# Transposing the attention probabilities of every second head pair on VectorE and through SBUF-to-SBUF transfers

## The chip, the cores and the metric

The kernel runs on one core of one Trainium2 chip. The metric is the device time of one execution in microseconds (us); the median of three runs of the kernel before is 1169.73 us (1169.29 to 1170.1).

## What is computed

A batch of four sequences of 512 tokens with 1024 features goes through a layer norm, a causal attention of 16 heads with rotary positions, and a gate from a feed-forward part with sign weights; the product of both is added to the input. Cut to the attention, which the change touches:

```python
xn = _layernorm(x, axis=-1)
q, k, v = ((xn @ w).reshape(b, s, 16, 64) for w in (Wq, Wk, Wv))
q, k = rotary(q), rotary(k)
logits = jnp.where(causal, einsum('bhqd,bhkd->bhqk', q, k), MASK_VAL) / 8
attn = softmax(logits, axis=-1)
out = einsum('bhqk,bhkd->bhqd', attn, v).reshape(b, s, e) @ Wo
...
x + out * silu(ffn(xn))
```

## The kernel before

**Units and groups.** A unit is a pair of heads of one sequence: 64 rows of q and k per head, 128 together. Two units make a group; there are four groups per sequence, 16 in all (`groups`, L225), numbered k = 0 to 15, with g = k mod 4 the place of a group in its sequence. The order of the work on TensorE (PE) is written out by hand (`manual_schedule`, L70). The order on the other engines is made by the framework's planner from the dependencies, with the order in which the instructions are traced as the priority. An instruction under `keep_in_program_order` is pinned behind the instruction of its engine that was traced just before it.

**The main loop** (L879 to L952) goes through the 16 groups. In the time of group k, PE does the projections of that group (queries, keys, values, each by a seven-product scheme; `fill`, a generator that gives one matmul at a time, 84 per group) and, between them, the attention of group k - 1. `interleave` (L870) takes a list of pieces, traces one, and then draws so many matmuls from `fill` that both lists end together: with 16 pieces that is 5.25 matmuls a piece. `attention_pieces` (L839) makes the list. In groups g = 2 and 3 the next sequence's layer norm is traced ahead of the pieces (`layernorm`, L915) and the transposes of its tokens are put among them (`extra`, L916). The first operations of the next sequence's sums (`form_x`, L298) are traced between the last group of one sequence and the first of the next (L951).

**Scores and softmax.** For the block row i of 128 queries, a score matmul (`scores`, L512) makes 128 x 128(i+1) logits per head in PSUM. VectorE (DVE) adds the mask on the diagonal block and takes the negated maximum (L528, L532), ScalarE (ACT) takes the exponential with the row sum (L535), VectorE the reciprocal (L543), and GpSimd (POOL) multiplies by it in place (L545). The score banks are `ps_sc`, two tiles of two banks each. `scores_1` does block row 1 of both units, `scores_3` row 3, `scores_02` rows 2 and 0. The probabilities lie in separate tiles for the rows 1, 3 and 2 with 0 (`new_probs`, L553), with 3, 2 and 2 buffers.

**Transposes and values.** The product with v needs the probabilities with keys on the partitions. `transpose_p` (L577) transposes four 128x128 blocks on PE into one PSUM bank; the five banks of a unit (20 blocks, `T_BANKS`) are copied to the tile `pT` by ScalarE (banks 0, 2, 4; L589) or VectorE (banks 1, 3; L587). `pT` comes from `ptp` (L144), a pool with one buffer. `values` (L591) then runs eight matmuls, VectorE copies the result from PSUM (L608), and a DMA issued on SyncE's queue (SP) stores it (L609). All banks of projections, transposes and values come from one ring of four PSUM banks (`ring`, L134).

**The order of the pieces.** `late` holds the two units of group k - 2, `w` and `v`: their scores were done in group k - 1's time, and their transposes and values are done in group k's. It is empty for k = 1. The list is five transposes of `w`; `scores_1` of the newer pair with the values of `w`; five transposes of `v`; `scores_3` with the values of `v`; a wait; `scores_02`; two waits (L858). The router's three steps (L617) are put in for g = 0.

**Queues.** Loads of weights and tokens, stores of tokens and values, and the router's small stores all stand in SP's queue, each behind its own waits.

**After the loop** (L1046 to L1094) the last two pairs' attention is mixed by hand with the feed-forward's matmuls (`dense`, L1050) and with `split` (L758), which works on ScalarE and VectorE. The rest, from 885 us on, is output projection and feed-forward, which the change leaves alone.

Of the kernel before, what the change touches and what calls it, by code (L numbers as in the profile page):

```python
# [9 lines left out]
F32 = mybir.dt.float32  # L10
# [10 lines left out]
B, S, E = 4, 512, 1024  # L21
H, D = 16, 64
NE = 8
P = 128
NT = B * S
NC = E // P
NPAIR = H // 2
NGRP = NPAIR // 2
TPB = S // P
# [4 lines left out]
SCALE = 0.125  # L34


T_BANKS = [
    [(0, 0, i) for i in range(4)],
    [(1, 0, i) for i in range(4)],
    [(0, 1, 1), (0, 1, 2), (0, 1, 3), (0, 3, 3)],  # L40
    [(1, 1, 1), (1, 1, 2), (1, 1, 3), (1, 3, 3)],
    [(0, 2, 2), (0, 2, 3), (1, 2, 2), (1, 2, 3)],
]


def t_place(h, j):

    return [(h, 0), (2 + h, 0), (4, 256 * h), (2 + h, 384)][j]


@with_exitstack
def attn_gated_ffn_kernel(
# [15 lines left out]
    nc = tc.nc  # L68
# [8 lines left out]
    ident = cp.tile([P, P], F32, name="ident")  # L77
# [4 lines left out]
        out=mask,  # L82
        in_=mask,
# [18 lines left out]
    osc = cp.tile([P, E], F32R, name="osc")  # L102
# [3 lines left out]
    for sign, base in ((1, 0), (-1, 7)):  # L106
        nc.gpsimd.affine_select(
            out=high,
# [45 lines left out]
    def bank(name):  # L154
        return ring.tile([P, S], F32, tag="r", name=name)
# [349 lines left out]

    def probs(u, i):

        if i % 2:
            return PR[u, i]
        return PR[u, 0][:, :, P * i // 2 : P * i // 2 + (i + 1) * P]  # L510

    def scores(blocks):  # L512

# [36 lines left out]
    def sc_bank(u, n):  # L550
        return ps_sc.tile([P, 2, S], F32, tag="sc", name="sc_%d_%d_%d_%d" % (*u, n))

    def new_probs(u, n, cols, bufs):  # L553
        PR[u, n] = pp.tile(
            [P, 2, cols], F32, tag=f"p{n}", name="p%d_%d_%d_%d" % (n, *u), bufs=bufs
        )

    def scores_1(units):
        ps = sc_bank(units[0], 1)
        for u in units:  # L560
            new_probs(u, 1, 2 * P, 3)
        scores([(u, 1, ps[:, :, n * TH : (n + 1) * TH]) for n, u in enumerate(units)])

    def scores_3(units):
        for u in units:
            new_probs(u, 3, S, 2)
        scores([(u, 3, sc_bank(u, 3)) for u in units])

    def scores_02(units):
        blocks = []  # L570
        for u in units:
            new_probs(u, 0, S, 2)
            ps = sc_bank(u, 0)
            blocks += [(u, 2, ps[:, :, P:]), (u, 0, ps[:, :, :P])]
        scores(blocks)

    def transpose_p(u, n):  # L577
        un = "%d_%d_%d" % u
        if u not in PT:
            PT[u] = ptp.tile([P, 5, S], F32, tag="pT", name=f"pT_{un}")  # L580
        tp = tp_bank(f"ptp_{un}_{n}")
        for k, (h, j, i) in enumerate(T_BANKS[n]):
            nc.tensor.transpose(tp[:, k, :], probs(u, i)[:, h, j * P : (j + 1) * P], ident)  # L583
        dst = PT[u][:, n, :]
        src = tp.rearrange("p j q -> p (j q)")
        if n % 2:
            nc.vector.tensor_copy(dst, src)  # L587
        else:
            nc.scalar.copy(dst, src)  # L589

    def values(u):  # L591
        b, g, i = u
        pr = g + NGRP * i
        pv = bank("pv_%d_%d_%d" % u)
        for j in range(TPB):
            for h in range(2):
                r = h * D
                n, o = t_place(h, j)
                nc.tensor.matmul(  # L599
                    pv[r : r + D, j * P :],  # L600
                    lhsT=V[u][:, j, r : r + D],
                    rhs=PT[u][:, n, o : o + (TPB - j) * P],
                    start=(j == 0),
                    stop=(j == TPB - 1),
                )

        at = V[u].rearrange("p t c -> p (t c)")
        nc.vector.tensor_copy(at, pv)  # L608
        nc.sync.dma_start(  # L609
            out=at_d[b].rearrange("t p (c q) -> p t c q", c=NC)[:, :, pr, :],  # L610
            in_=at.rearrange("p (t q) -> p t q", t=TPB),
        )


# [224 lines left out]
    def attention_pieces(k, late):  # L839

        units = [(*groups[k], i) for i in range(2)]
        w, v = late

        def pt(u):
            return [lambda n=n: transpose_p(u, n) for n in range(5)] if u else []

        def with_values(scores_of, u):
            def both():
                scores_of(units)
                if u:  # L850
                    values(u)

            return both

        def wait():
            pass

        pieces = [  # L858
            *pt(w),
            with_values(scores_1, w),  # L860
            *pt(v),
            with_values(scores_3, v),
            wait,
            lambda: scores_02(units),
            wait,
            wait,
        ]
        return pieces, units

    def interleave(pieces, fill, n_fill):  # L870
# [8 lines left out]
    for k, (b, g) in enumerate(groups):  # L879
# [4 lines left out]
        if g == 0:  # L884
            routing = [lambda n=n: router(b, n) for n in range(3)]
            if k == 0:
                nothing = lambda: None
                pieces = [
                    routing[0],
                    lambda: (load_scales(in_scale), load_scales(out_scale)),  # L890
                    routing[1],
                    nothing,
                    routing[2],
                    lambda: split_scales(isc),
                    nothing,
                    nothing,
                    nothing,
                ]
            else:

                if b < B - 1:
                    pieces.insert(7, routing[0])
                pieces.insert(10, routing[1])
                pieces.insert(13, routing[2])
        elif g == 1 and b + 1 < B:

            pieces.insert(12, lambda: [load_x(b + 1, t) for t in range(2)])
            if b == 0:
                pieces.insert(6, lambda: split_scales(osc))

                pieces.insert(1, lambda: None)
        elif g > 1 and b + 1 < B:
            t0 = 2 * (g - 2)
            for t in range(t0, t0 + 2):
                layernorm(b + 1, t)  # L915
            extra = [  # L916
                lambda t=t, h=h: transpose_x(b + 1, t, h) for t in range(t0, t0 + 2) for h in range(2)
            ]
            if g == 2:
                extra.append(lambda: [load_x(b + 1, t) for t in (2, 3)])  # L920

        step = max(1, (len(pieces) + len(extra)) // (len(extra) + 1))
        for n, e in enumerate(extra):
            pieces.insert(min(len(pieces), (n + 1) * step + n), e)
        if len(pieces) > 18:

            pieces.append(lambda: None)
        if k in (5, 9, 12, 13):
            n = {5: 0, 9: 2, 12: 4, 13: 6}[k]
            pieces.insert(8, lambda: make_sign(n + 1))  # L930
# [116 lines left out]
    w, v = late  # L1047
    sums = iter([(n, c) for n in (1, 3) for c in range(4)])

    def dense(gates, n):  # L1050
        for _ in range(n):
            next(gates)
            if n > 1:
                nxt = next(sums, None)
                if nxt:
                    sum_wo(*nxt)

    for n in range(5):
        transpose_p(w, n)
    split(0, 0)  # L1060
    scores_1(units)
    split(0, 1)
    values(w)
    gates = gated(0)
    for ns in ((0, 1), (2, 3), (4,)):
        dense(gates, 2)
        for n in ns:
            transpose_p(v, n)
    scores_3(units)
    values(v)  # L1070
    dense(gates, 6)

    split(1, 0)
# [348 lines left out]
```

## Time and profile before

| | |
|---|---|
| median of three runs | 1169.73 us |
| the profiled execution | 1170.42 us, its span 1168.6 us |
| granted TensorE clock | 0.998 |
| PE busy in the span | 1159.0 us |
| DVE, ACT, POOL busy in the span | 826.0, 496.8, 559.8 us |
| projections on PE, share of the chain that ended last | L342 31%, L429 15% |
| transposes of probabilities, scores, values, share of the chain | 6%, 6%, 6% |
| DVE, ACT, POOL busy in the group from 354 to 406 us | 37.7, 27.7, 26.6 us of 52 |
| bytes moved by DMA | 121.92 MB, mean 104 GB/s |

The span is the time from the first to the last instruction on the core. PE is TensorE's matmul side and PEld its weight loads. A row of the groups names the line, the engine, the operation and the tiles (out<-in with shapes and a count), then the busy time in total, the mean duration of one in ns, and the idle time of the engine just before. A row of the timeline gives the start, the length and the merged instructions. A row of waits gives who waited for whom, with the sum, the number and the longest. A float32 matmul stands as two instructions in the trace, a transpose as one. Numbers like 128x256 are partitions by elements.

### The profile page before, as it was taken

What the parts mean: (1) busy time and instruction counts of PE and PEld (TensorE: products, weight loads), DVE (VectorE), ACT (ScalarE), POOL (GpSimd) and SP (SyncE); (2) the same over time, 40 slices, a digit from 0 to 9 for tenths busy, and PEclk for the clock granted to TensorE, in tenths of its full rate; (3) what the DMA queues carried; (4) which work ended last, traced back from release to release, by engine and by line L of the source; (5) the groups of instructions that cost most, each with busy time, mean ns of one, the idle gap of its engine ahead of it and who ended that gap; (6) DMA issues with size and microseconds to landing.
All of it is one profiled execution on the core that took longest, in us unless ns stands there. A gap on an engine that the chain in (4) does not pass through costs nothing.

```text
span 1168.6 us, 16127 instructions
## 1 busy us (share of the span) xinstructions
PE 1159.0 (99%) x5816; PEld 851.2 (73%) x5816; DVE 826.0 (71%) x1452; ACT 496.8 (43%) x1132; POOL 559.8 (48%) x590
## 2 busy tenths in 40 slices
PE   9999999999999999999999999999999999999998
PEld 8887787878778787877878787877775455545554
DVE  7866686677767667776867776675768786677664
ACT  2552664354356444534743563364442131223121
POOL 0661554355246435623642654264465554454435
PEclk9999999999999999999999999999999999999999
DMA  8412522322242141223236221220603424332331
GB/s 311 134 37 90 162 82 67 133 84 82 81 132 103 54 153 50 98 100 118 81 91 226 84 73 58 78 82 14 216 15 108 130 95 145 112 95 100 135 108 54
DMA packets 62319, 121.92 MB, mean 104 GB/s; under 512 B 5280, under 2 KB 40864, under 8 KB 56224
## 3 DMA queue, kind: packets, MB, share of 16 engines
q1 hardware_dynamic: 57376, 112.11, 28.6%
q0 software_dynamic: 4576, 8.39, 2.1%
q8 instruction: 46, 0.75, 0.2%
q10 hardware_dynamic: 288, 0.39, 0.1%
q14 instruction: 33, 0.27, 0.1%
HBM read 95.45 MB, written 25.43 MB: 103 GB/s over the span
## 4 chain that ended last, share of the span: by engine, by line
PE 92%; DVE 3%; ACT 2%; issue 1%; POOL 1%; POOLq 0%; DVEq 0%; ACTq 0%
PE pj L342 31%; PE wo L1243 15%; PE pj L429 15%; PE ff L1183 7%; PE pv L599 6%; PE sc L517 6%; PE ptp L583 6%; PE ff L1004 3%; PE xtp L210 1%; ACT p L535 1%; PE idle L793 1%; DVE S L296 1%; PE lg L622 1%; DVE w L296 1%; ACT sw L324 1%
## 5 line engine op out<-in xcount | busy, mean ns | idle before, releaser
L545 POOL TENSOR_SCALAR p<-p,rs 128x128 f32<-128x128 f32 (+3 forms) x256 | 171.2, 682 | 265.6 <-DVE rs L543 265.5
L535 ACT ACTIVATE p<-sc,nmx 128x128 f32<-128x128 f32 (+3 forms) x256 | 132.7, 524 | 158.9 <-DVE nmx L532 151.4
L342 PE MATMUL pj<-X,w 128*128 128x256 f32 x576 | 138.3, 381 | 0.2 <-ACT X L216 0.2
L326 POOL TENSOR_TENSOR sw<-sw,sin_sb 128x512 f32<-128x512 f32 x64 | 87.5, 1367 | 94.8 <-ACT sw L324 79.0
L342 PE MATMUL pj<-T,S 128*128 128x256 f32 x512 | 123.4, 382 | 0.1
L342 PEld LDWEIGHTS pj<-X,w 128*128 128x128 f32 x576 | 105.1, 190 | 14.4 <-issue 1.8
L342 PE MATMUL pj<-T,w 128*128 128x256 f32 x448 | 107.6, 381 | 0.0
L589 ACT COPY pT<-ptp 128x512 f32<-128x512 f32 x96 | 56.2, 586 | 120.3 <-PE ptp L583 119.9
L532 DVE TENSOR_REDUCE nmx<-sc 128x2 f32<-128x512 f32 (+3 forms) x128 | 103.7, 821 | 2.9
L342 PEld LDWEIGHTS pj<-T,S 128*128 128x128 f32 x512 | 93.3, 190 | 13.0 <-issue 0.4
L429 PE MATMUL pj<-w,X 128*128 128x256 f32 x416 | 99.6, 386 | 2.6 <-DVE w L296 2.6
L327 POOL TENSOR_TENSOR rot<-rot,sw 128x512 f32<-128x512 f32 x64 | 93.7, 1464 | 4.7
L583 PE MATMUL ptp<-ident,p 128*128 128x128 f32 x640 | 94.8, 273 | 0.3 <-ACT pT L589 0.3
L323 ACT ACTIVATE sw<-c 32x512 f32<-32x512 f32 x128 | 80.4, 628 | 34.6 <-DVE c L356 32.6
L583 PEld LDWEIGHTS ptp<-ident,p 128*128 128x128 f32 x640 | 79.0, 141 | 16.5 <-DVE pT L587 0.9
L342 PEld LDWEIGHTS pj<-T,w 128*128 128x128 f32 x448 | 82.1, 190 | 11.4 <-issue 1.8
L429 PEld LDWEIGHTS pj<-w,X 128*128 128x128 f32 x416 | 77.7, 193 | 14.0 <-DVE w L296 3.0
L517 PE MATMUL sc<-rot,rot 64*128 64x384 f32 (+3 forms) x512 | 82.0, 449 | 0.0
L429 PE MATMUL pj<-w,T 128*128 128x256 f32 x352 | 81.8, 383 | 0.0
L324 ACT ACTIVATE sw<-c 32x512 f32<-32x512 f32 x128 | 80.4, 628 | 1.7
L599 PE MATMUL pv<-pT,v 128*64 128x256 f32 (+3 forms) x512 | 76.0, 439 | 0.0
L528 DVE TENSOR_TENSOR sc<-sc,mask 128x256 f32<-128x256 f32 x128 | 53.8, 420 | 28.7 <-PE sc L517 28.4
(180 smaller groups left out, 2086.5 us busy)
## 6 DMA issues: line engine op xcount, KB each, us to landing
w<-in_wqk SPq DMA_DIRECT2D x31, 1024.0 KB, 5.2
w<-in_wv SPq DMA_DIRECT2D x16, 1024.0 KB, 4.8
x<-in_x SPq DMA_DIRECT2D x16, 512.0 KB, 3.7
xn_d<-X SPq DMA_DIRECT2D x16, 512.0 KB, 5.8
at_d<-v SPq DMA_DIRECT2D x32, 256.0 KB, 2.3
xp<-xn_d SPq DMA_DIRECT2D x16, 512.0 KB, 4.8
ap<-at_d SPq DMA_DIRECT2D x16, 512.0 KB, 4.9
xr<-in_x SPq DMA_DIRECT2D x32, 256.0 KB, 2.8
```

The lines of the kernel that those rows point to most:

```text
L324: nc.scalar.activation(sw[r + 32 : r + 64, :], c[r : r + 32, :], AF.Copy, scale=sc)
L326: nc.gpsimd.tensor_tensor(sw, sw, sin_sb, op=ALU.mult)
L327: nc.gpsimd.tensor_tensor(rot, rot, sw, op=ALU.add)
L342: nc.tensor.matmul(ps, lhsT=wq[:, k, :], rhs=xq[:, k, :], start=(k == 0), stop=(k == 3))
L429: nc.tensor.matmul(ps[:, j, :], lhsT=xq[:, k, j * P : (j + 1) * P], rhs=wq[:, k, :], start=(k == 0), stop=(k == 3),)
L517: nc.tensor.matmul(ps[:, h, :], lhsT=Q[u][r : r + D, i * P : (i + 1) * P], rhs=K[u][r : r + D, : (i + 1) * P], start=True, stop=True,)
L532: nc.vector.tensor_reduce(nmx, ps, AX.X, ALU.max, negate=True)
L535: nc.scalar.activation(pt[:, h, :], ps[:, h, :], AF.Exp, bias=nmx[:, h : h + 1], accum_out=ssum[:, h : h + 1],)
L545: nc.gpsimd.tensor_scalar(pt[:, h, :], pt[:, h, :], rs[:, h : h + 1], 1.0, op0=ALU.mult, op1=ALU.mult,)
L583: nc.tensor.transpose(tp[:, k, :], probs(u, i)[:, h, j * P : (j + 1) * P], ident)
L599: nc.tensor.matmul(pv[r : r + D, j * P :], lhsT=V[u][:, j, r : r + D], rhs=PT[u][:, n, o : o + (TPB - j) * P], start=(j == 0), stop=(j == ...
L1243: nc.tensor.matmul(ps, lhsT=lhs[:, k, :], rhs=rhs[:, k, :], start=(first and k == 0), stop=(k == 3), skip_group_check=not first,)
```

## The change

Four things are done together.

- **`w` without PE.** `transpose_blocks` transposes the probabilities of `w` on VectorE, ten instructions for the ten block pairs (both heads at once), each a 4x4 grid of separate 32x32 transposes, into a tile y; sixteen DMAs on SP's queue then move the 32-row strips of y to their places, into the unit's own probability buffer. y has the tag `pT`, so it takes the one buffer that the transposed probabilities of `v` take afterwards. The ten instructions are pinned in program order.
- **A new layout.** A unit's transposed probabilities are stored as four strips of 640 columns, each with 32 queries of every block. `transpose_p` (for `v`, and for both units in the tail) copies its banks into that layout, bank 4 by two copies of half the size. `values` reads and writes with that order of columns, and its copy from PSUM is made by ScalarE, which puts the columns back in order.
- **One probability buffer per unit** of 10 x 128 columns a head, two buffers in all, in place of three tiles. The new pair's `scores_1` can take these buffers when the old pair is done with them.
- **New pieces.** 16 pieces for k from 2: 0 the block transposes of `w`; 6, 7, 8 the PE transposes of `v`; 9 the values of `w` and `v` and then `scores_1`; 12 `scores_3`; 14 `scores_02`. The router's steps move to pieces 1, 3 and 5, the split of the scales in k = 1 to piece 1. In the tail the values of both units come ahead of `scores_1`, and the dense matmuls that stood between the transposes of `v` come after.

```diff
--- before.py
+++ after.py
@@ -34,18 +34,17 @@
 SCALE = 0.125
 
 
+
+QCOL = [0, P, 3 * P, 6 * P]
+OFF = [0, 128, 256, 224]
+
 T_BANKS = [
-    [(0, 0, i) for i in range(4)],
-    [(1, 0, i) for i in range(4)],
-    [(0, 1, 1), (0, 1, 2), (0, 1, 3), (0, 3, 3)],
-    [(1, 1, 1), (1, 1, 2), (1, 1, 3), (1, 3, 3)],
-    [(0, 2, 2), (0, 2, 3), (1, 2, 2), (1, 2, 3)],
+    [(0, 0, [(0, i) for i in range(4)])],
+    [(1, 0, [(0, i) for i in range(4)])],
+    [(0, OFF[1], [(1, 1), (1, 2), (1, 3), (3, 3)])],
+    [(1, OFF[1], [(1, 1), (1, 2), (1, 3), (3, 3)])],
+    [(h, OFF[2], [(2, 2), (2, 3)]) for h in range(2)],
 ]
-
-
-def t_place(h, j):
-
-    return [(h, 0), (2 + h, 0), (4, 256 * h), (2 + h, 384)][j]
 
 
 @with_exitstack
@@ -505,9 +504,7 @@
 
     def probs(u, i):
 
-        if i % 2:
-            return PR[u, i]
-        return PR[u, 0][:, :, P * i // 2 : P * i // 2 + (i + 1) * P]
+        return PR[u][:, :, QCOL[i] : QCOL[i] + (i + 1) * P]
 
     def scores(blocks):
 
@@ -550,65 +547,93 @@
     def sc_bank(u, n):
         return ps_sc.tile([P, 2, S], F32, tag="sc", name="sc_%d_%d_%d_%d" % (*u, n))
 
-    def new_probs(u, n, cols, bufs):
-        PR[u, n] = pp.tile(
-            [P, 2, cols], F32, tag=f"p{n}", name="p%d_%d_%d_%d" % (n, *u), bufs=bufs
-        )
+    def new_probs(u):
+        PR[u] = pp.tile([P, 2, 10 * P], F32, tag="p", name="p_%d_%d_%d" % u)
 
     def scores_1(units):
         ps = sc_bank(units[0], 1)
         for u in units:
-            new_probs(u, 1, 2 * P, 3)
+            new_probs(u)
         scores([(u, 1, ps[:, :, n * TH : (n + 1) * TH]) for n, u in enumerate(units)])
 
     def scores_3(units):
-        for u in units:
-            new_probs(u, 3, S, 2)
         scores([(u, 3, sc_bank(u, 3)) for u in units])
 
     def scores_02(units):
         blocks = []
         for u in units:
-            new_probs(u, 0, S, 2)
             ps = sc_bank(u, 0)
             blocks += [(u, 2, ps[:, :, P:]), (u, 0, ps[:, :, :P])]
         scores(blocks)
 
+    def by_place(t):
+        return t.rearrange("p (a n) -> p a n", a=4)
+
+    def transpose_blocks(u):
+
+
+        y = ptp.tile([P, 20 * P], F32, tag="pT", name="y_%d_%d_%d" % u)
+        out = by_place(y).rearrange("p b (h n) -> p h b n", h=2)
+        for j in range(TPB):
+            for i in range(j, TPB):
+                src = probs(u, i)[:, :, j * P : (j + 1) * P]
+                o = OFF[j] + 32 * (i - j)
+                tc.keep_in_program_order(
+                    nc.vector.transpose(
+                        out[:, :, :, o : o + 32], src.rearrange("p h (b c) -> p h b c", b=4)
+                    )
+                )
+
+        PT[u] = by_place(PR[u].rearrange("p h n -> p (h n)"))
+        for a in range(4):
+            for b in range(4):
+                nc.sync.dma_start(
+                    out=PT[u][32 * b : 32 * b + 32, a, :],
+                    in_=by_place(y)[32 * a : 32 * a + 32, b, :],
+                )
+
     def transpose_p(u, n):
         un = "%d_%d_%d" % u
-        if u not in PT:
-            PT[u] = ptp.tile([P, 5, S], F32, tag="pT", name=f"pT_{un}")
+        if n == 0:
+            PT[u] = by_place(ptp.tile([P, 20 * P], F32, tag="pT", name=f"pT_{un}"))
         tp = tp_bank(f"ptp_{un}_{n}")
-        for k, (h, j, i) in enumerate(T_BANKS[n]):
-            nc.tensor.transpose(tp[:, k, :], probs(u, i)[:, h, j * P : (j + 1) * P], ident)
-        dst = PT[u][:, n, :]
-        src = tp.rearrange("p j q -> p (j q)")
-        if n % 2:
-            nc.vector.tensor_copy(dst, src)
-        else:
-            nc.scalar.copy(dst, src)
+        k = 0
+        for h, o, blocks in T_BANKS[n]:
+            first = k
+            for j, i in blocks:
+                nc.tensor.transpose(tp[:, k, :], probs(u, i)[:, h, j * P : (j + 1) * P], ident)
+                k += 1
+            o += 320 * h
+            dst = PT[u][:, :, o : o + 32 * len(blocks)]
+            dst = dst.rearrange("p a (k q) -> p k a q", q=32)
+            src = tp[:, first:k, :].rearrange("p k (a q) -> p k a q", q=32)
+            if n % 2:
+                nc.vector.tensor_copy(dst, src)
+            else:
+                nc.scalar.copy(dst, src)
 
     def values(u):
         b, g, i = u
         pr = g + NGRP * i
-        pv = bank("pv_%d_%d_%d" % u)
+        pv = by_place(bank("pv_%d_%d_%d" % u))
         for j in range(TPB):
             for h in range(2):
                 r = h * D
-                n, o = t_place(h, j)
+                o = 320 * h + OFF[j]
                 nc.tensor.matmul(
-                    pv[r : r + D, j * P :],
+                    pv[r : r + D, :, 32 * j :],
                     lhsT=V[u][:, j, r : r + D],
-                    rhs=PT[u][:, n, o : o + (TPB - j) * P],
+                    rhs=PT[u][:, :, o : o + 32 * (TPB - j)],
                     start=(j == 0),
                     stop=(j == TPB - 1),
                 )
 
-        at = V[u].rearrange("p t c -> p (t c)")
-        nc.vector.tensor_copy(at, pv)
+        at = V[u]
+        nc.scalar.copy(
+            at.rearrange("p t (a q) -> p t a q", q=32), pv.rearrange("p a (t q) -> p t a q", q=32)
+        )
         nc.sync.dma_start(
-            out=at_d[b].rearrange("t p (c q) -> p t c q", c=NC)[:, :, pr, :],
-            in_=at.rearrange("p (t q) -> p t q", t=TPB),
+            out=at_d[b].rearrange("t p (c q) -> p t c q", c=NC)[:, :, pr, :], in_=at
         )
 
 
@@ -841,30 +866,28 @@
         units = [(*groups[k], i) for i in range(2)]
         w, v = late
 
-        def pt(u):
-            return [lambda n=n: transpose_p(u, n) for n in range(5)] if u else []
-
-        def with_values(scores_of, u):
-            def both():
-                scores_of(units)
-                if u:
-                    values(u)
-
-            return both
-
-        def wait():
+        def nothing():
             pass
 
-        pieces = [
-            *pt(w),
-            with_values(scores_1, w),
-            *pt(v),
-            with_values(scores_3, v),
-            wait,
-            lambda: scores_02(units),
-            wait,
-            wait,
-        ]
+        def both_values():
+            for u in late:
+                values(u)
+            scores_1(units)
+
+        pieces = [nothing] * 16
+        if w:
+
+            pieces[0] = lambda: transpose_blocks(w)
+            pieces[6] = lambda: [transpose_p(v, n) for n in (0, 1)]
+            pieces[7] = lambda: [transpose_p(v, n) for n in (2, 3)]
+            pieces[8] = lambda: transpose_p(v, 4)
+            pieces[9] = both_values
+            pieces[12] = lambda: scores_3(units)
+            pieces[14] = lambda: scores_02(units)
+        else:
+            pieces[0] = lambda: scores_1(units)
+            pieces[6] = lambda: scores_3(units)
+            pieces[10] = lambda: scores_02(units)
         return pieces, units
 
     def interleave(pieces, fill, n_fill):
@@ -898,17 +921,15 @@
                 ]
             else:
 
+                pieces[5], pieces[3] = routing[2], routing[1]
                 if b < B - 1:
-                    pieces.insert(7, routing[0])
-                pieces.insert(10, routing[1])
-                pieces.insert(13, routing[2])
+                    pieces[1] = routing[0]
         elif g == 1 and b + 1 < B:
 
             pieces.insert(12, lambda: [load_x(b + 1, t) for t in range(2)])
             if b == 0:
-                pieces.insert(6, lambda: split_scales(osc))
-
-                pieces.insert(1, lambda: None)
+
+                pieces.insert(1, lambda: split_scales(osc))
         elif g > 1 and b + 1 < B:
             t0 = 2 * (g - 2)
             for t in range(t0, t0 + 2):
@@ -922,9 +943,6 @@
         step = max(1, (len(pieces) + len(extra)) // (len(extra) + 1))
         for n, e in enumerate(extra):
             pieces.insert(min(len(pieces), (n + 1) * step + n), e)
-        if len(pieces) > 18:
-
-            pieces.append(lambda: None)
         if k in (5, 9, 12, 13):
             n = {5: 0, 9: 2, 12: 4, 13: 6}[k]
             pieces.insert(8, lambda: make_sign(n + 1))
@@ -1058,16 +1076,15 @@
     for n in range(5):
         transpose_p(w, n)
     split(0, 0)
+    values(w)
+    for n in range(5):
+        transpose_p(v, n)
+    split(0, 1)
+    values(v)
     scores_1(units)
-    split(0, 1)
-    values(w)
     gates = gated(0)
-    for ns in ((0, 1), (2, 3), (4,)):
-        dense(gates, 2)
-        for n in ns:
-            transpose_p(v, n)
+    dense(gates, 6)
     scores_3(units)
-    values(v)
     dense(gates, 6)
 
     split(1, 0)
```

## The prediction

> **What bounds the kernel now.** I read the page's head first: PE is busy for 1159.0 of 1168.6 us, in all but the last of the 40 slices. Then the waits, with PE as the waiting engine, to see whether that busy time is a queue without holes:
>
> ```profile
> span 1168.6 us, 16127 instructions
> PE 1159.0 (99%) x5816; PEld 851.2 (73%) x5816; DVE 826.0 (71%) x1452; ACT 496.8 (43%) x1132; POOL 559.8 (48%) x590
> ```
> ```profile
> PE pj L429 <- DVE w L296: 2.6, 1, 2.6
> ...
> PE ptp L583 <- ACT pT L589: 0.3, 1, 0.3
> ```
>
> Five such waits exist, 4.9 us in all. So time is won only by giving PE less to do, and lost wherever PE is made to wait. The chain of waits says the same (PE 92%, `ptp L583` 6%).
>
> What a transpose costs PE is not in the groups view: its mean of 273 ns is a latency with a modelled end. The timeline shows the pitch, in the gap from the first transpose of a bank to the first projection matmul after it:
>
> ```profile
> 171.09 0.60 PE L583 MATMUL ptp<-ident,p 128*128 128x128 f32 x4
> 171.52 1.89 PE L429 MATMUL pj<-w,X 128*128 128x256 f32 x8
> 173.25 0.60 PE L583 MATMUL ptp<-ident,p 128*128 128x128 f32 x4
> 173.69 1.89 PE L429 MATMUL pj<-w,X 128*128 128x256 f32 x8
> ```
>
> Four transposes take 171.52 - 171.09 = 0.43 us, 0.108 each; eight projection instructions (four matmuls, two instructions each) take 1.73 us, 0.432 a matmul. These two numbers give all times on PE below. The other engines' part is in the groups by shape:
>
> ```profile
> L589 ACT COPY pT<-ptp 128x512 f32<-128x512 f32 x96 | 56.2, 586 | 120.3 <-PE ptp L583 119.9
> L587 DVE COPY pT<-ptp 128x512 f32<-128x512 f32 x64 | 43.7, 684 | 18.8 <-PE ptp L583 18.7
> L608 DVE COPY v<-pv 128x512 f32<-128x512 f32 x32 | 21.8, 680 | 11.6 <-PE pv L599 11.6
> L455 DVE TENSOR_TENSOR v<-pj,v 128x256 f32<-128x256 f32 x64 | 23.8, 410 | 2.8 <-PE pj L429 2.8
> ```
>
> [...]
>
> **The change, part by part.**
>
> PE's work removed. Only groups with a pending pair have a `w`: k = 2 to 15, 14 units. Each loses 20 transposes: 14 x 20 x 0.108 = **-30.2 us** on PE, all of it on the path. Scores, values and projections keep their counts. Values now read and write in runs of 32 columns; no row shows such a matmul, so 0 is the least; a tenth on 32 units at 2.3 us (16 `pv` instructions from 166.95 to 169.26) would be 7 us. I take 0[...].
>
> VectorE. It loses 28 copies at 0.684 and 32 evictions of values at 0.680, 41 us; it gains 140 transposes of 128x256. The nearest row is L455, 0.41 us, pairs of it 0.38 apart in the timeline[...]. At 0.38 a unit takes 3.8 us, 53 in all. So +12 on an engine busy for 37 of 52 us a group: hidden as a sum. ACT loses 42 copies (25 us), gains 32 evictions (about 19) and 18 split copies (about 3): hidden.
>
> The transfers are what matters. y has the tag and the single buffer of the transposed probabilities. So the copies of `v`'s first bank (piece 6) wait until all 16 transfers of `w` have read y, not merely the values (piece 9). PE goes on with at most two banks held, since its ring has four: it blocks at the fourth bank of `v`, about 0.4 us into piece 7. On PE's clock from the start of a group: with 16 pieces a piece holds 5.25 matmuls, 2.27 us, so the block is at 6 x 2.27 + 0.87 + 2.27 + 0.43 = 17.1. With the four extra pieces of g = 3 it is 16.5 (30 matmuls, one bank of x, then 0.87, 4 matmuls, 0.43), with the five of g = 2 17.7.
>
> When do the transfers land? The steps are: start of the transposes; 3.8 us for them; 16 issues on SP; the last landing; 0.7 for the first copy. An issue that has another behind it is long: four of 32 rows took 1.72 us, 0.43 each, so 6.9. [...] The last lands about 1.4 us after its issue (small ones here: 1.7 to 2.2 from the beginning of issue). Sum after the start: 3.8 + 6.9 + 1.4 + 0.7 = 12.8 us.
>
> The start is the open term. Two things hold it: the probabilities of block 0, and the pinning: the first transpose stays behind whatever VectorE instruction was traced before it. For the probabilities:
>
> ```profile
> 351.51 2.00 PE L517 MATMUL sc<-rot,rot 64*128 64x384 f32 x16
> ...
> 358.82 1.15 POOL L545 TENSOR_SCALAR p<-p,rs 128x128 f32<-128x128 f32 x2 [0.46 <-DVE rs L543]
> ...
> 361.76 0.60 PE L583 MATMUL ptp<-ident,p 128*128 128x128 f32 x4
> ```
>
> They are ready 8 us after `scores_02` begins, which now stands two pieces before the boundary (about 6.5 us), so at about +2. Then 2 + 12.8 = 14.8: in time for 17.1. That serves k = 5, 9 and 13 to 15: **no wait**. In k = 4, 8, 12 the operation ahead is the fourth `form_x`, ending 3.9 after the boundary: 16.7, just in time.
>
> In g = 2 and 3 of the first three batches the operation ahead is the second `normalize`, since `layernorm` is traced ahead of the pieces:
>
> ```profile
> 363.53 1.28 DVE L180 BATCH_NORM_STATS2 bn<-x 128x6 f32<-128x512 f32 x2
> ...
> 367.71 0.81 DVE L196 TENSOR_SCALAR x<-x,mv,rstd 128x1024 f32<-128x1024 f32 x1
> ...
> 372.53 1.03 DVE L196 TENSOR_SCALAR x<-x,mv,rstd 128x1024 f32<-128x1024 f32 x1
> ```
>
> Here, in k = 7, it ends 11.8 us after the boundary at 361.76 (k = 3 the same), in k = 6 and 10 8.2, in k = 2 5.5. The chain gets shorter, as copies of `pT` that stood in it go (two in k = 7, one in k = 6, 0.6 to 0.7 each) and ACT has fewer copies ahead of the square roots (I take 1 us in g = 3): 9.6 and 7.5. So k = 3, 7, 11: 9.6 + 12.8 = 22.4 against 16.5, 5.9 each, **+17.7**; k = 6, 10: 20.3 against 17.7, 2.6 each, **+5.2**; k = 2 in time. The stall does not pass on: what VectorE and POOL owe PE catches up in it.
>
> While the transposes stand at the head of VectorE, `add`, `form_w` and the router's small operations queue behind them, for some 4 us and the wait for POOL. PE waits for these evictions, but has four banks at 3.5 us each: nothing taken. SP's later loads of w stand behind the 16 issues; they were issued over one key ahead, so nothing. The output DMAs on POOL are not passed.
>
> The tail. `v`'s five banks follow `values(w)` without the dense matmuls that lay between them, and `pT` has one buffer: the copies wait for the last read, while ACT and VectorE have the splits too. The work on PE between covers most; I take **+1** (0 to 4).
>
> Sum: -30.2 + 17.7 + 5.2 + 1 = -6.3. The profiled execution took 1170.4 (span 1168.6 and 1.8 around it), 0.7 over the median of 1169.7. So 1169.7 - 6.3 = **1163**.
>
> **Rivals.**
> *The cover holds.* VectorE gets to its `normalize` sooner than I think, or the issues take the lone 0.33 us of the w loads (5.3 for 16). With no wait at all: 1169.7 - 30.2 + 1 = 1141; with a third of the wait left, 1148. For it speaks that most groups have 2 us to spare; against it the chain of k = 7, measured three times alike.
> *The transfers land later: slower.* Place: `v`'s first copy in g = 2 and 3. Chains as in before (11.8, 8.2, 5.5) and 0.52 an issue, as `xn_d` takes: 1.4 us more for 16. k = 3, 7, 11: 26.0 against 16.5, 28.5 in all; k = 6, 10: 22.4 against 17.7, 9.4; k = 2: 2; k = 4, 8, 12: 1 each, 3. Waits of 43: 1169.7 - 30.2 + 43 + 1 = 1184. It decides from 29 us of waits. [...]
> *Two-pass transposes*, the dear end: 3.8 us more in each group, waits of about 63: 1204. [...]
>
> **How the numbers follow.** Forecast 1163 (1156 to 1167): 0.40. Cover holds, 1141 to 1155: 0.15. Later landing, 1172 to 1190: 0.30. Dearer still, up to 1204 and beyond: 0.08. Between, within 0.2% (2.3 us, about what a measurement of this kernel can tell from no change): 0.07. So faster 0.55, same 0.07, slower 0.38. The range 1144 to 1189 leaves out the best of the second case and the dearest.
>
> **What would show it.** PE's `ptp` count falls from 640 to 360 at the same pitch. VectorE shows 140 transposes near 0.38 us. SP shows 224 more issues near 0.43. PE's waits show `ptp` behind ACT's copy of `pT`, and that behind a DMA, in k = 3, 7, 11 for about 6 us and hardly in k = 5 or 13. It is wrong if these waits stand in all groups alike (transposes or issues dear), if there are none, or if PE waits at the values or for projection banks instead.

## The result and the profile after

The change makes the kernel slower: 1258.6 us (median of four runs, 1256.8 to 1262.2) against 1169.9 before on the same chip, a ratio of 1.0763 with a 95% interval of 1.0738 to 1.0788. That is 89 us more, where 7 us less were forecast.

The page's head of the kernel after, with the granted TensorE clock in 40 slices:

```profile
span 1260.5 us, 16085 instructions
...
PE 1165.6 (92%) x5536; PEld 842.8 (67%) x5536; DVE 842.8 (67%) x1532; ACT 498.1 (40%) x1144; POOL 548.4 (44%) x590
...
PEclk9998989998989899998979999999999999999999
```

PE has 280 instructions less and is no longer busy throughout: 95 us of the span are idle. Its clock was 9 in every slice of the kernel before; now eight of the first 21 slices, all of them in the loop, show 8 or 7. The line of before:

```profile
PEclk9999999999999999999999999999999999999999
```

The waits with PE as the waiting engine (who waits for whom: sum, number, longest):

```profile
PE ptp L604 <- ACT pT L613: 29.7, 23, 7.9
PE ptp L604 <- DVE c L355: 12.1, 6, 3.0
PE ptp L604 <- ACT part L449: 11.0, 4, 4.2
PE pj L428 <- DVE part L355: 6.4, 2, 3.2
PE xtp L209 <- DVE x L195: 4.6, 4, 2.2
```

Only the first row was forecast. In the next three VectorE or ScalarE is late with an eviction, that is, a copy out of a PSUM bank; the fourth row is a wait at a projection bank, which the prediction had named as a sign of being wrong. In the last row the layer norm's rows are late. None of the four names a transfer, but the second hangs on the shared buffer all the same: in own_y below, which gives y a buffer of its own, 0.8 of its 12.1 us are left. The others stay for the most part. The copies that themselves wait for a transfer are these:

```profile
DVE pT L611 <- DMA p<-y: 28.1, 6, 8.8
ACT pT L613 <- DMA p<-y: 17.9, 7, 5.0
```

They stand in k = 2, 3, 6, 7, 10 and 11, and with 0.2 us in k = 4. The transposes in the groups by shape, and the transfers among the DMA issues (count, size, median us to landing):

```profile
L582 DVE STREAM_TRANSPOSE y<-p 128x256 f32<-128x256 f32 x140 | 48.5, 406 | 2.7 <-POOL p L542 2.5
```
```profile
p<-y SPq DMA_DIRECT2D x224, 80.0 KB, 2.1
```

The dear groups are those with g = 3. The timeline of k = 7, which begins at 391.5:

```profile
403.93 1.37 DVE L195 TENSOR_SCALAR x<-x,mv,rstd 128x1024 f32<-128x1024 f32 x1
405.23 3.37 DVE L582 STREAM_TRANSPOSE y<-p 128x256 f32<-128x256 f32 x10
408.53 0.38 DVE L355 TENSOR_TENSOR part<-pj,part 128x256 f32<-128x256 f32 x1
...
408.66 10.82 SPq L590 DMA_DIRECT2D p<-y  x16
...
408.96 1.47 PE L428 MATMUL pj<-w,X 128*128 128x256 f32 x4 [3.20 <-DVE part L355]
...
414.48 0.60 PE L604 MATMUL ptp<-ident,p 128*128 128x128 f32 x4
421.70 1.11 PE L604 MATMUL ptp<-ident,p 128*128 128x128 f32 x4 [6.62 <-ACT pT L613]
422.61 3.62 PE L428 MATMUL pj<-w,X 128*128 128x256 f32 x8
...
426.79 1.89 PE L428 MATMUL pj<-w,X 128*128 128x256 f32 x8
428.52 0.38 PE L604 MATMUL ptp<-ident,p 128*128 128x128 f32 x2
429.36 0.44 PE L604 MATMUL ptp<-ident,p 128*128 128x128 f32 x2 [0.46 <-ACT pT L613]
```

Four losses can be read here. PE waits 3.2 us for an eviction (`part`) that stands behind the ten transposes, which stand behind the second `normalize`. At the fourth bank of `v` it waits 6.6 us for the copy that needs the buffer of y. The eight projection instructions that follow it take 3.4 us (from 422.61 to 426.02, where a row left out here begins), the eight from 426.79 on 1.73. And between the two halves of bank 4 there are 0.5 us.

The whole difference can be added up from the intervals between the starts of PE's matmuls. The pitch is the usual interval for a matmul of its shape, and a hold is what PE waits beyond it. From k = 0 to the end of the loop 818.2 us became 902.8. Holds ahead of a matmul rose from 3.5 to 91.8 us; what intervals without such a hold were over the pitch (slow matmuls) rose from 13.0 to 38.4; what is left, the work itself, fell by 29. After the loop 332.8 became 340.1. That makes 92, the difference of the spans.

### The profile page after: what moved, and what is told of

It reads as the page before. It is cut to its first block, busy times and chain, and to the rows that moved or that the text cites. A ratio compares the mean times of both kernels' runs of the same rounds, so it can differ in the third digit from the quotient of the medians.

```text
span 1260.5 us, 16085 instructions
## 1 busy us (share of the span) xinstructions
PE 1165.6 (92%) x5536; PEld 842.8 (67%) x5536; DVE 842.8 (67%) x1532; ACT 498.1 (40%) x1144; POOL 548.4 (44%) x590
## 4 chain that ended last, share of the span: by engine, by line
PE 59%; DVE 16%; ACT 9%; SPq 5%; issue 5%; POOL 2%; DMA 2%; POOLq 0%; ACTq 0%; DVEq 0%
PE pj L341 14%; PE wo L1260 13%; PE pj L428 10%; PE ff L1200 6%; PE pv L623 5%; SPq L590 5%; PE sc L514 4%; ACT p L532 4%; DVE y L582 3%; DVE nmx L529 3%; PE ptp L604 3%; DVE S L295 2%; PE ff L1022 2%; ACT sw L323 2%; ACT sw L322 1%
## 5 line engine op out<-in xcount | busy, mean ns | idle before, releaser
L542 POOL TENSOR_SCALAR p<-p,rs 128x128 f32<-128x128 f32 (+3 forms) x256 | 165.7, 660 | 336.1 <-DVE rs L540 311.8
L341 PE MATMUL pj<-X,w 128*128 128x256 f32 x576 | 134.8, 381 | 3.9 <-DVE pT L611 3.7
L428 PE MATMUL pj<-w,X 128*128 128x256 f32 x416 | 111.9, 422 | 8.5 <-DVE part L355 6.4
L604 PE MATMUL ptp<-ident,p 128*128 128x128 f32 x360 | 61.8, 304 | 61.6 <-ACT pT L613 29.7
L341 PEld LDWEIGHTS pj<-T,S 128*128 128x128 f32 x512 | 99.0, 198 | 21.9 <-ACT pT L613 3.8
L428 PEld LDWEIGHTS pj<-w,X 128*128 128x128 f32 x416 | 85.9, 213 | 24.1 <-DVE part L355 7.2
L604 PEld LDWEIGHTS ptp<-ident,p 128*128 128x128 f32 x360 | 46.0, 155 | 79.4 <-ACT pT L613 35.8
L326 POOL TENSOR_TENSOR rot<-rot,sw 128x512 f32<-128x512 f32 x64 | 90.7, 1418 | 4.9
L391 POOL TENSOR_TENSOR part<-part,part 128x256 f32<-128x256 f32 x32 | 26.3, 823 | 127.4 <-ACT part L390 90.3
L428 PEld LDWEIGHTS pj<-w,T 128*128 128x128 f32 x352 | 65.7, 190 | 13.8 <-PE sc L514 3.0
```

The source lines that it names most:

```text
L326: nc.gpsimd.tensor_tensor(rot, rot, sw, op=ALU.add)
L341: nc.tensor.matmul(ps, lhsT=wq[:, k, :], rhs=xq[:, k, :], start=(k == 0), stop=(k == 3))
L428: nc.tensor.matmul(ps[:, j, :], lhsT=xq[:, k, j * P : (j + 1) * P], rhs=wq[:, k, :], start=(k == 0), stop=(k == 3),)
L542: nc.gpsimd.tensor_scalar(pt[:, h, :], pt[:, h, :], rs[:, h : h + 1], 1.0, op0=ALU.mult, op1=ALU.mult,)
```

## The experiments

Two theories stood against each other. *Buffer*: the copies of `v` wait for the 16 transfers of `w`, as forecast, only longer. *Backlog*: VectorE and ScalarE fall behind the block transposes and the bunched pieces, whatever becomes of the transfers. The expectations below call the first A; they split the second into B, the new order of pieces, and C, VectorE's transposes. Each diff is against the kernel after unless another is named, and leaves out lines at the dots and at its end.

**A buffer of its own for y.** Every kernel whose name begins with own_y makes room for it by letting two pairs of the gate's tables share storage, so its gate has other values.

```diff
-    osc = cp.tile([P, E], F32R, name="osc")
+    osc = isc
...
+    yp = right(name="blocksT", bufs=1)
...
-        y = ptp.tile([P, 20 * P], F32, tag="pT", name="y_%d_%d_%d" % u)
+        y = yp.tile([P, 20 * P], F32, tag="y", name="y_%d_%d_%d" % u)
```

> The block transposes' tile y gets a buffer of its own (room for it is made by letting two constant tables share storage, so the gate's values differ from the reference's; the instructions keep their number and shape). Theory A, PE waits because v's first copy may not start before the 16 transfers have read the shared buffer: those waits go, what is left is the values of w in g = 3, about 5 us each, so 1165 to 1195 us. Rival B, the new order of pieces and the single probability buffers cost the time: no change, 1245 or more. Rival C, VectorE's transposes at the head of its queue hold up the projections' evictions: 1225 or more.

1202.8 us, ratio 1.0286 (1.0267 to 1.0305), in none of the three ranges: the shared buffer is worth 56 of the 89. By groups, the three with g = 2 win 5 to 6 us each and k = 3, 7 and 11 win 6 to 10, together 43. The others win 0 to 4 each, 14 in all, though the trace names no wait of over 0.2 us for a transfer there. But 33 us remain over the kernel before and 63 over the forecast without holds, so *buffer* alone fails. No copy of `pT` waits for a transfer any more, and PE's largest waits are now these (the first row now also counts what is left of the wait for ScalarE's `part`):

```profile
PE ptp L606 <- ACT pT L615: 24.6, 27, 3.3
PE pj L430 <- DVE part L357: 6.4, 2, 3.2
PE xtp L211 <- DVE x L197: 4.2, 4, 1.9
```

**Fewer or quicker transfers, buffer still shared.** In four_strips only the four strips that stay in their rows (a = b) are moved, and the values of `w` come from what then lies there; in two_queues all 16 are, issued by SyncE and GpSimd in turn. The two edits, one after the other:

```diff
-            for b in range(4):
+            for b in (a,):
...
-                nc.sync.dma_start(
+                (nc.sync, nc.gpsimd)[b % 2].dma_start(
```

> Only 4 of the 16 transfers of a unit are issued (the diagonal strips), the others are left out, so the values of w are computed from partly untransposed probabilities. Theory A with the issue on SP as the step that was too small: the last transfer lands 7.6 us sooner (12 x 0.63), the waits in g = 0, 1, 2 go, g = 3 keeps about 5 us each: 1160 to 1190 us. Rival C (VectorE): 1225 or more, since the transposes stay.

> The kernel after, but the 16 transfers of a unit are issued alternately by SyncE and GpSimd. If the 10 to 11.6 us of issuing on one queue set the landing, the last strip lands about 5 us sooner and the holds in all groups shrink: 1215 to 1235. If the transfers themselves (32 rows on a side) are the limit, the landing stays and so does the time: 1250 or more.

1210.6 us (1.0339, 1.0322 to 1.0356), between the two ranges, and 1219.2 (1.0423, 1.0407 to 1.0438), as expected. With two queues the 16 issues take 5.9 to 6.8 us in place of 10.0 to 11.6, though a transfer then needs 3.4 us to land in place of 2.1; in k = 2, 3, 4, 6 and 7 the last strip lands, and the first copy of `v` begins, 2.5 to 4.4 us sooner. So issuing on one queue is a large part of what sets the landing, though less than the 5 us expected. Even with a quarter of the transfers the time stays 8 us above a buffer of its own.

**The order alone.** `w` is transposed on PE again, in pieces 0, 2 and 4, with its values at 4; no block transposes and no transfers between buffers.

```diff
-            for u in late:
-                values(u)
+            values(v)
...
-            pieces[0] = lambda: transpose_blocks(w)
+            pieces[0] = lambda: [transpose_p(w, n) for n in (0, 1)]
+            pieces[2] = lambda: [transpose_p(w, n) for n in (2, 3)]
+            pieces[4] = lambda: (transpose_p(w, 4), values(w))
```

> w is transposed on PE again (pieces 0, 2, 4, its values at the end of piece 4), in the new layout, with the new buffers and the new places of v, scores and tail: no VectorE transposes, no transfers. Theory A: PE has its 30 us back but no late transfers: 1170 to 1190 us, of it about 7 from the tail. Rival B (order and buffers cost): 1258 + 30 less what DMA waits share, so 1250 to 1290.

1231.2 us (1.0528, 1.0512 to 1.0543), between the two ranges and far over the first: with as many matmuls as before, the new order costs 61 us, so it is dear even without the new path. PE's waits say where:

```profile
PE ptp L604 <- POOL p L542: 20.4, 8, 5.6
PE ptp L604 <- ACT pT L613: 16.8, 32, 1.8
```

`scores_02` now stands two pieces ahead of the boundary, so its probabilities come up to 5.6 us late for a transpose in piece 0. In this kernel PE waits for them, in the kernel after VectorE does (2.5 us in all). And ScalarE's copies of `pT` stop PE 32 times, by 0.5 us in the mean, most of it at bank 4.

**Bank 4.** Its two half copies are traced after its four transposes, in place of one after every two.

```diff
         for h, o, blocks in T_BANKS[n]:
-            first = k
             for j, i in blocks:
                 nc.tensor.transpose(tp[:, k, :], probs(u, i)[:, h, j * P : (j + 1) * P], ident)
                 k += 1
+        k = 0
+        for h, o, blocks in T_BANKS[n]:
+            first = k
+            k += len(blocks)
             o += 320 * h
```

> The kernel after, but the four transposes of bank 4 are all traced ahead of its two half copies. Half copies stop PE for about 0.6 us once in each of the 18 units transposed on PE: if that is a term of its own, 1243 to 1249. If PE's hold at bank 4 is only the end of the hold for the buffer y, it stays at 1257 to 1259.

1252.3 us (1.0704, 1.0673 to 1.0735): 6 us, half of what was expected. 18 times 0.63 are 11; but k = 12 became 4.4 us longer, 1.2 of them as a hold at the router's transposes grew there from 2.0 to 3.2 us. The other 3.2 were not separated.

**VectorE's share.** own_y with one of the ten block transposes.

```diff
-        for j in range(TPB):
-            for i in range(j, TPB):
+        for j in range(1):
+            for i in range(1):
```

> own_y with one of the ten block transposes per unit left out of nothing but VectorE's queue: nine of ten are not done (y is one tile, cleared once), the 16 transfers stay; the values of w are computed from that. If the 3.4 us on VectorE in each group make its evictions late, it is about 20 us under own_y, 1180 or less. If VectorE is no cause: about 1200.

1183.8 us (1.0119, 1.0104 to 1.0134), 19 us under own_y: 14 units win 1.4 us each in the mean from 3 us less on VectorE. (Their transfers can start sooner as well, but no copy waits for a transfer in either kernel.) How so little gets so far is seen in the kernel after at k = 5, in the timeline:

```profile
278.86 3.36 DVE L582 STREAM_TRANSPOSE y<-p 128x256 f32<-128x256 f32 x10
282.14 0.38 DVE L355 TENSOR_TENSOR c<-pj,part 128x256 f32<-128x256 f32 x1
...
291.47 0.41 DVE L355 TENSOR_TENSOR c<-pj,part 128x256 f32<-128x256 f32 x1
...
291.92 0.63 ACT L322 ACTIVATE sw<-c 32x512 f32<-32x512 f32 x1 [5.10 <-DVE c L355]
...
297.06 0.59 ACT L449 COPY part<-pj 128x512 f32<-128x512 f32 x1
297.54 0.59 ACT L613 COPY pT<-ptp 128x512 f32<-128x512 f32 x1
...
297.70 1.97 PE L604 MATMUL ptp<-ident,p 128*128 128x128 f32 x8 [4.25 <-ACT part L449]
```

VectorE is busy from 278.86 to 294.95, with no gap of over 0.04 us. Its eviction `c` at 291.47 is late; ScalarE idles 5.1 us for it and then runs the eight rotary copies `sw`, 0.63 each, ahead of `part` and `pT`. PE, which has sent two banks of `v` close together, has no bank left and waits 4.25 us. The last packet of the strips had ended at 293.5, as the hold begins: no transfer is in this chain. With a buffer of its own for y this group takes 56.3 us in place of 58.8, and the hold 3.0: most of it stays. What it wins comes from ScalarE's queue, in which the planner then puts the first copy of `pT` behind six of the eight `sw` and ahead of `part`, here in own_y:

```profile
277.42 0.59 ACT L615 COPY pT<-ptp 128x512 f32<-128x512 f32 x1
```

So the shared buffer also costs where nothing waits for a transfer, through the order that the planner makes.

**Spreading the banks of `v`.** own_y, with bank 4's copies joined and one bank a piece:

```diff
-            pieces[6] = lambda: [transpose_p(v, n) for n in (0, 1)]
-            pieces[7] = lambda: [transpose_p(v, n) for n in (2, 3)]
-            pieces[8] = lambda: transpose_p(v, 4)
-            pieces[9] = both_values
+            for n in range(5):
+                pieces[6 + n] = lambda n=n: transpose_p(v, n)
+            fourth = pieces[10]
+            pieces[10] = lambda: (fourth(), both_values())
```

> own_y (y in a buffer of its own; room is made by letting the second scale matrix and one sign matrix be those of another, so the gate's values differ), with bank 4's copies joined behind its four transposes, and the five banks of v one in each of the pieces 6 to 10, both values at 10. If what is left in own_y is the bunching of two banks a piece in front of a late VectorE and ScalarE: 1175 to 1190. If it is PE waiting for probabilities or for layer norm's rows: about 1195.

1174.5 us (1.0041, 1.0026 to 1.0056), 28 less than own_y. Two banks a piece in a ring of four, ahead of engines that are late, was the second large cause; bank 4, worth 6 us in the kernel after, is in the 28 and was not separated here.

**The layer norm's place.** Traced behind the block transposes; first in the kernel after, then in own_y_spread with the token transposes moved later too.

```diff
-            for t in range(t0, t0 + 2):
-                layernorm(b + 1, t)
+            first = pieces[0]
+            pieces[0] = lambda: (first(), [layernorm(b + 1, t) for t in range(t0, t0 + 2)])
```

In own_y_norm also:

```diff
-            pieces.insert(min(len(pieces), (n + 1) * step + n), e)
+            pieces.insert([8, 10, 14, 17, 20][n] if len(extra) > 3 else min(len(pieces), (n + 1) * step + n), e)
```

> As the changed kernel, but the layer norm of the next sequence is traced after the block transposes and not ahead of them. Theory A with the pinning as the cause of the long waits in g = 3: the transposes there start 8 us sooner, three groups win 8 to 12 us each with the clock: 1222 to 1236 us. If the pinning is not it, or the layer norm then makes the transposes of x late instead: 1250 or more.

> own_y_spread (1174.5), but in g = 2 and 3 the next sequence's layer norm is traced behind the block transposes, and the token transposes that read it stand later among the pieces (after about half of them). In own_y_spread the three groups g = 3 are still 3 to 6 us longer than in the kernel before, with a hold of 3.4 us at 13.6 us behind the pinned transposes. If the pinning behind layer norm is that term: 1164 to 1168. If the hold only moves to the token transposes, as it did in norm_later: 1172 or more.

The first, 1249.8 us (1.0678, 1.0662 to 1.0694), misses the range that was hoped for: k = 3, 7 and 11 win 4 to 5 us each, but PE loses much of what the sooner transfers bring at the token transposes, whose rows now come late (27.1 us in place of 4.6):

```profile
PE xtp L209 <- DVE x L195: 27.1, 6, 5.7
```

With those moved as well it is 1166.9 us (0.9962, 0.9949 to 0.9975), 8 less than own_y_spread and faster than before.

**The tail, the places of the scores, and VectorE once more.** own_y_best is own_y_norm with dense matmuls between the banks of `v` in the tail again; own_y_late is own_y_norm with the banks at 7 to 11 and the scores at 11, 13, 15 in place of 10, 12, 14; own_y_late_few leaves out nine of ten block transposes of own_y_late. The edits of the first two:

```diff
+    for ns in ((0, 1), (2, 3), (4,)):
+        dense(gates, 2)
+        for n in ns:
+            transpose_p(v, n)
...
-                pieces[6 + n] = lambda n=n: transpose_p(v, n)
+                pieces[7 + n] = lambda n=n: transpose_p(v, n)
...
-            pieces[12] = lambda: scores_3(units)
-            pieces[14] = lambda: scores_02(units)
+            pieces[13] = lambda: scores_3(units)
+            pieces[15] = lambda: scores_02(units)
```

> own_y_norm, and after the loop two of the feed-forward's dense pieces stand again between the banks of v. If the tail's +5.5 us come from the five banks standing back to back: 5 us less than own_y_norm, 1159 to 1163. If not: the same as own_y_norm.

> own_y_norm (1166.9) with the banks of v in the pieces 7 to 11 and the scores at 11, 13 and 15 in place of 6 to 10 and 10, 12, 14. In own_y_norm PE's score matmuls take 81.3 us in the loop against 73.7 before, as they wait for the exponentials of the scores ahead of them, and k = 15 holds for 2.3 us. If the places of the scores cause that: 1159 to 1163. If it is only VectorE and ScalarE being busy: 1166 to 1168.

> own_y_late with one of the ten block transposes of each unit (nine are not done, the transfers stay, y is one tile cleared once). If the 3.4 us on VectorE still make evictions late when the banks are spread: 6 to 12 us under own_y_late. If the spread has hidden them: within 2 us of own_y_late.

own_y_best takes 1167.4 us (0.9973, 0.9963 to 0.9983): nothing, so the tail's theory falls. own_y_late takes 1163.5 (0.9943, 0.9928 to 0.9957): 3 us less than own_y_norm, just outside the expected range, and as the two intervals overlap the 3 us are not certain. own_y_late_few takes 1156.6 (0.9886, 0.9871 to 0.9901): VectorE's 3 us a unit still cost 7 in all when the banks are spread.

**In the memory of the kernel after.** The same findings with y in its shared buffer: two queues, bank 4 joined, `v` in the pieces 7 to 11, values at 11, scores at 11, 13, 15 (two_spread); layer norm and token transposes later as well, with the interleaved tail (two_best) or with the tail of the change and the router's steps at 3, 6 and 12 (two_router). What two_router adds to two_spread, beside the later layer norm:

```diff
-                pieces[5], pieces[3] = routing[2], routing[1]
+                pieces[12], pieces[6] = routing[2], routing[1]
                 if b < B - 1:
-                    pieces[1] = routing[0]
+                    pieces[3] = routing[0]
```

> The kernel after with its shared buffer, the transfers on two queues, bank 4's copies joined, the five banks of v one in each of the pieces 7 to 11, both values at 11, scores at 11, 13 and 15. If the shared buffer costs only because its first copy comes too early and the banks are bunched: near own_y_spread, 1178 to 1190. If the shared buffer holds PE in any order: 1205 or more.

> two_spread with the later layer norm and the interleaved tail of own_y_best. It computes all of the reference in the same memory as the kernel after. If the terms add: 10 to 15 us less than two_spread, about 1165 to 1178, so near the kernel before (1170).

> two_spread with the later layer norm, the tail of the kernel after, and the router's steps at pieces 3, 6 and 12, behind the evictions that follow the block transposes. It computes all of the reference. two_best (1176.4) holds 6.2 us in all at the router's transposes: 1168 to 1173 if that hold goes, 1176 if it only moves.

1181.9 us (1.0100, 1.0085 to 1.0115), 1176.4 (1.0050, 1.0035 to 1.0065) and 1169.9 (0.9998, 0.9991 to 1.0006). So all 89 us are won back without more memory, and PE's idle time in the loop falls from 82 us to 23; but that is the time before, no less. Of the 6.5 us between two_best and two_router 5.9 lie after the loop (345.3 against 339.4), so most of them belong to the interleaved tail and not to the router's steps. The largest sums among its waits are small and scattered:

```profile
PE sc L514 <- ACT p L532: 4.0, 4, 1.0
PE ptp L603 <- DVE part L355: 3.8, 3, 2.7
PE ptp L603 <- DVE c L355: 3.3, 2, 1.6
```

No version that computes all of the reference beats both kernels. own_y_late, 0.6% faster than before, shows what a buffer more would bring; room for it was only made by sharing other tables.

## Why the prediction was wrong, step by step

- **PE's saving** was right. 280 transposes went; in the loop they had taken 61.6 us of PE's intervals, in own_y_late_few 32.1 are left. The strided values cost nothing, as taken: 62.4 us against 64.5.
- **The block transposes** were right: 3.4 us a unit in the median (3.36 to 4.22) against 3.8, an estimate from additions of the same size. In k = 5 and 7 the ten follow each other at 0.33 us, as the pairs of additions do (the 0.38 of the forecast is half of a row of two, of 0.75 us), so the two passes of the rival, 7.6 us a unit, are excluded.
- **The issues** were mis-sized: 10.0 to 11.6 us for 16 against 6.9, so 0.63 each and not the 0.43 of the four router stores. Per strip of 80 KiB that is 130 GB/s.
- **The start** was mis-sized. The forecast asked when the probabilities of `w` are ready, about +2. But the transposes are pinned behind the instruction traced last, the reciprocal of the *second* unit's block 0, in k = 5 at 278.78 (+4.7). In g = 3 the `normalize` ended at +13.8 in k = 7 and not at 9.6; it ended later than before, not sooner.

| from the group's start, us | k = 5 | k = 6 | k = 7 |
|---|---|---|---|
| transposes begin, forecast and measured | 2, 4.8 | 7.5, 6.1 | 9.6, 13.8 |
| last strip lands (measured: end of its last packet), forecast and measured | 14.1, 19.4 | 19.6, 21.6 | 21.7, 29.2 |
| holds of PE, forecast and measured | 0, 6.9 | 2.6, 5.2 | 5.9, 13.0 |

- **The hold at the buffer** was the right mechanism, mis-sized: own_y prices the shared buffer at 56 us where 22.9 were forecast. Copies wait for the strips in the five groups that were forecast and in k = 2, and those six give 43 of the 56; the others come through the planner's order, as at k = 5. Part of the price was not in the forecast's sum: behind a hold PE can be slow. The eight projection instructions after the hold of 6.6 us took 3.4 us against 1.73, and the granted clock from 421.7 to 426.8 was 0.51. In the whole loop the slow intervals rose by 25 us, from 13 to 38; own_y has 22 of them. 16 of the 38 stand right behind the eight holds of 3.2 us or more. Others stand behind shorter ones, as in k = 6, where eight projection instructions from 355.87 on are 0.43 us apart in place of 0.22, at a granted clock of 0.50, after holds of 3.0 and 1.1 us; what brought those on was not settled.
- **"Nothing taken" for VectorE's queue is the step that failed beside that size**, and with it the silence on the new order of pieces: PE's four banks were counted as cover for the evictions behind the transposes, while the same four were counted to hold banks of `v`. Two banks a piece used them up. That is most of the 63 us by which own_y is over the forecast without holds: the bunching 28 (own_y to own_y_spread, bank 4 included), the pinning behind layer norm 8, the scores' places 3 (not certain), the transposes on VectorE 7, and 17 more that stand below. VectorE's share hangs on the order, 19 us in own_y and 7 in own_y_late. The sum of busy times (+12 forecast, +17 measured) told nothing of it.
- **Bank 4's split copies** were counted as ScalarE's time only. They stop PE, which in this kernel writes the second half of the bank only when ScalarE has read the first: PE starts at 429.36, as ScalarE's copy of the first half, from 428.94 on with 0.37 us, ends. It is 0.63 a unit over the pitch, and joining the copies won 6 us.
- **The tail** was +1 and came out +7.3. 2.5 of it stand at the half copies (bank4's tail is 337.6 us against 340.1), 2.6 at waits for the probabilities and exponentials of the last units, 2.3 in the first 72 instructions of the output projection, 1.2 of them a wait for one of VectorE's sums. Interleaving it did not help; why these waits came was not settled.
- **The rivals.** Later landing was right in its mechanism and nearer in its prices (0.52 an issue where 0.63 was measured, 11.8 us to the end of the `normalize` of k = 7 where it was 13.8), and it named k = 2. It ended at 1184 because it too had nothing for VectorE, the order of pieces and the slow PE after a hold. Two-pass transposes and a cover that holds are excluded.

From own_y_late_few down to the forecast's 1139.5 (1169.7 less 30.2) 17 us are left: the tail's 8, 5.7 in which score matmuls wait for exponentials (79.4 us against 73.7), and small holds. They were not separated further.

## What to carry to other kernels

When work is taken off a bound engine, ask for each buffer that hides something what else the change counts on it for: here four banks were spent twice. An instruction pinned at the head of a queue starts when its *predecessor* ends (in k = 5 at +4.8 us where +2 was forecast), so look up what was traced last, for both units of a pair. Here 3.4 us on an engine that is busy for 67% of the span led to a hold of 4.25 us in k = 5, as eight rotary copies of 0.63 us on another engine hung on what was behind them; and with 88 us more of holds came 25 us more of slow matmuls.

## What the runs showed of the hardware

Back-to-back transfers of 32 rows by 2560 bytes inside SBUF took 0.63 us each on one queue (16 in 10.0 to 11.6 us); on two queues the 16 took 5.9 to 6.8 us to issue and each transfer 3.4 us to land in place of 2.1, and in k = 2, 3, 4, 6 and 7 the last still landed 2.5 to 4.4 us sooner. A block transpose of 128x256 float32 on VectorE has a pitch of 0.33 us (k = 5 and 7 of the kernel after), less than its mean row of 406 ns. After a hold of 6.6 us eight projection instructions took 3.4 us in place of 1.73, at a granted clock of 0.51.
